# A graph network kernel: the in-degree product made inside the third tile period, a large accumulator for the last tile's gate product, and its gated rows converted at once

## The chip, the cores and the metric

The kernel runs on one core of a Trainium2 chip. The metric is the device time of one execution in microseconds (us); the time before is the median of three runs, 2218.25 us (2213.3 to 2223.8). The profile is of one further execution, of 2215.67 us; its span, from the first to the last recorded instruction, is 2213.9 us.

## The reference, cut to what matters

625 nodes have rows of 1024 numbers, and 10000 edges lead from `src` to `dst`. Two blocks follow each other, each a graph layer plus a linear attention, then a feed-forward part:

```
x = x + gat(ln(x)) + linear_attention_0(ln(x))
x = x + ternary_ffn(ln(x))                  # int8-like rows, three-valued weights
x = x + sage(ln(x)) + linear_attention_1(ln(x))
x = x + attention_and_experts(ln(x))
```

Two pieces matter here. The three-valued feed-forward part (`_L0_ffn_ref`) makes, for every row, a gate and an up product of 256 columns each from the rounded row, multiplies silu(gate) by up, rounds the result again, and multiplies it by `w_down`. The second graph layer (`_L1_gnn_ref`) takes a mean over incoming edges, so it needs `deg`, the count of edges into each node, and `1 / max(deg, 1)`.

## The kernel before, in words

All rows stay on the chip as five tiles (`NT = 5`) of 125 rows (`P`). The edges are turned once into a matrix of counts, `CT`, with sources on partitions and destinations along the free axis (626 columns, of which the last is padding). Right after it is made, one is added on its diagonal for the self-loops of the first graph layer.

The order of work is written out by hand: within the manual schedule each engine executes its instructions in the order in which the Python code emits them. The helper `do(prep, pe, after, after2)` (class `Stream`, line 189) emits first the waiting `after` steps of earlier calls, one step of each, and then the TensorE work `pe` of this call. So what evacuates a product is emitted one `do` later than the product, and a second step, `after2`, two later. Nearly all TensorE products are emitted by the helper `group`, so the profile gives them line 137 and they are told apart by the name of their accumulator.

PSUM is split into two kinds of accumulator: two small ones of one bank (`ps1`, line 63) and three large ones of two banks (`ps2`, line 67). A tile that is asked for waits on the chip until the earlier user of its buffer has been read.

The change lies in the loop over tile periods, `for p in range(NT + 2)` (line 1076), periods 0 to 6, called the first to the seventh here. It interleaves the first graph layer's softmax-weighted sums (`sums`, `turn_sums`, `up_again`) of tile p, the feed-forward part of tile p-1 (`ffn`, returning the steps p1, f1, f2, f3, f4, p5, f5) and the layer norm and transposition of tile p-2 (p5, f5, into `xnT1`). The steps of `ffn` are: p1 statistics and rounding; f1 eight transposes into `ptr`; f2 the gate and up product `pgu` and, one `do` later, tanh on ScalarE and the gated rows `sg` on VectorE; f3 two transposes into `phT` and, one `do` later, the conversion into `hT` (line 1017; the profile calls the shared tile that holds xq, qT, sg and hT `room`); f4 the product `pdn`, and one `do` later its addition into `x` (line 1033); p5 the next layer's norm (line 1040); f5 eight transposes (line 1048) and two ScalarE copies into `xnT1` (line 1049). `spacer` (line 1065) puts in between a key or value product of the second block's linear attention (`pk`, `pv`), which use large accumulators. A key product is followed by a VectorE addition `kb` (line 272), two ScalarE steps (`ke`, `kb`, lines 274 and 275), and as `after2` a VectorE step `kf` (line 280) that waits for them.

During the third period two large accumulators hold the unfinished output projections of tiles 2 and 4 (`px`), and the third one passes from `pdn` to the next user.

After the loop comes the second block's linear attention. Between two of its products `degrees()` (line 1143) takes the diagonal off `CT` again (five VectorE instructions), multiplies a matrix of ones by `CT` into `pdeg` (TensorE, 20 records in the profile), and one `do` later makes `dinv = max(degree, 1)` from `pdeg` and two checks: no count is over 4094, and the counts add up to the number of edges. If a check of this kind fails, the kernel runs its whole work once more in a slower form. `inverses()` then takes reciprocals.

Of the kernel before, what the change touches and what calls it, by code (L numbers as in the profile page):

```python
# [8 lines left out]
FP = mybir.dt.float32  # L9
# [4 lines left out]
AF = mybir.ActivationFunctionType  # L14
ALU = mybir.AluOpType
AX = mybir.AxisListType
# [3 lines left out]
N = 625  # L20
NT = 5
P = 125
NP = 626
HN = 313
E = 10000
# [13 lines left out]
MAGIC = 12582912.0  # L39
# [14 lines left out]
def attempt(ctx: ExitStack, tc: tile.TileContext, w: dict, out: bass.AP, shifted: bool):  # L54

    nc = tc.nc
# [6 lines left out]
    def ps1(name):  # L63
        pool, n = psums[-1]
        return pool.tile([128, 512], FP, tag="ps1", name=name, bufs=n)

    def ps2(name):
        return psums[-1][0].tile([128, 2, 512], FP, tag="ps2", name=name, bufs=3)


    ident = const.tile([128, 128], FP, name="ident")
# [5 lines left out]
    ones = const.tile([128, 128], FP, name="ones")  # L77
# [6 lines left out]
    inside = const.tile([128, 4], FP, name="inside")  # L84
# [49 lines left out]
    def group(dst, pairs):  # L134

        for i, (lhsT, rhs) in enumerate(pairs):
            made = nc.tensor.matmul(dst, lhsT=lhsT, rhs=rhs, start=(i == 0), stop=(i == len(pairs) - 1))  # L137
        latest["pe"] = made.ins.name
# [16 lines left out]
    def halves(ap):  # L155
        return ap.rearrange("p (h n) -> p h n", h=2)

    def nodes(t):
        return slice(t * P, (t + 1) * P)
# [26 lines left out]
    CT = CTr if shifted else CTr.bitcast(FP)  # L186
# [30 lines left out]
    mix = mixed_up.enter_context(tc.tile_pool(name="mix", bufs=1))  # L217
# [4 lines left out]
    do = Stream()  # L222
    hold = {}
# [139 lines left out]
    with ExitStack() as st0:  # L363
# [600 lines left out]
        def ffn(t):  # L964

            room = late.tile([128, 1536], FP, tag="room", name="room", bufs=1)
            xq = room[:P, 0:D]
            qT = room[:, D:D + KC * 64].bitcast(BF).rearrange("p (k n) -> p k n", k=KC)
            sg = room[:P, 0:256]
            hT = room[:, 256:384].bitcast(BF).rearrange("p (k n) -> p k n", k=2)  # L970
            xn1 = [mix.tile([128, NP], FP, tag="qf", name="xn1", bufs=2)[:P, 0:512] for h in range(2)]

            def p1():
                stats(t, mv0, rs0)
                nc.vector.tensor_scalar(xq, x[:, t, :], mv0[:, t, 0:1], rs0[:, t:t + 1],
                                        op0=ALU.subtract, op1=ALU.mult)
                quantise(xq, xq, rx[:, t:t + 1])

            def f1():
                def pe():  # L980
                    for h in range(2):
                        p = ps1("ptr").rearrange("p (c n) -> p c n", c=4)
                        for c in range(4):
                            k = 4 * h + c
                            nc.tensor.transpose(p[:, c, :P], xq[:, k * 128:(k + 1) * 128], ident[:P, :P])
                        nc.vector.tensor_scalar(qT[:, 4 * h:4 * h + 4, 0:P], p[:, :, :P], MAGIC, None,
                                                op0=ALU.subtract)

                do(None, pe)

            def f2():
                def pe():
                    hold["pgu"] = ps1("pgu")
                    group(hold["pgu"][:P], [(qT[:, k, 0:P], gu[:, k, :]) for k in range(KC)])

                def after():
                    pgu = hold["pgu"]
                    rgu = late.tile([P, 2], FP, tag="rgu", name="rgu", bufs=2)

                    nc.vector.tensor_scalar(rgu, wmean[:P, 0:2], rx[:, t:t + 1], None, op0=ALU.mult)  # L1000
                    nc.vector.tensor_scalar(rgu[:, 0:1], rgu[:, 0:1], 0.5, None, op0=ALU.mult)
                    nc.scalar.activation(sg, pgu[:P, 0:256], AF.Tanh, scale=rgu[:, 0:1])
                    nc.vector.scalar_tensor_tensor(sg, sg, 1.0, pgu[:P, 0:256], op0=ALU.add, op1=ALU.mult)
                    nc.vector.tensor_tensor(rgu[:, 1:2], rgu[:, 0:1], rgu[:, 1:2], op=ALU.mult)
                    nc.vector.scalar_tensor_tensor(sg, pgu[:P, 256:512], rgu[:, 1:2], sg, op0=ALU.mult, op1=ALU.mult)
                    quantise(sg, sg, rh[:, t:t + 1])

                do(None, pe, after)

            def f3():  # L1010
                def pe():
                    hold["ph"] = ps1("phT").rearrange("p (c n) -> p c n", c=4)
                    for c in range(2):
                        nc.tensor.transpose(hold["ph"][:, c, :P], sg[:, c * 128:(c + 1) * 128], ident[:P, :P])

                def after():
                    nc.vector.tensor_scalar(hT[:, :, 0:P], hold["ph"][:, 0:2, :P], MAGIC, None, op0=ALU.subtract)

                do(None, pe, after)

            def f4():
                def pe():
                    hold["pdn"] = ps2("pdn")
                    for c in range(2):
                        group(hold["pdn"][:P, c, :], [(hT[:, k, 0:P], dn[:, k, c * 512:(c + 1) * 512])
                                                   for k in range(2)])

                def after():
                    rd = late.tile([P, 1], FP, tag="rd", name="rd", bufs=2)
                    nc.vector.tensor_scalar(rd, wmean[:P, 2:3], rh[:, t:t + 1], None, op0=ALU.mult)  # L1030
                    for c in range(2):
                        xc = x[:, t, c * 512:(c + 1) * 512]
                        nc.vector.scalar_tensor_tensor(xc, hold["pdn"][:P, c, :], rd, xc, op0=ALU.mult, op1=ALU.add)

                do(None, pe, after)

            def p5():
                stats(t, mv1, rs1)
                for h in range(2):
                    nc.vector.tensor_scalar(xn1[h], x[:, t, h * 512:(h + 1) * 512], mv1[:, t, 0:1], rs1[:, t:t + 1],  # L1040
                                            op0=ALU.subtract, op1=ALU.mult)

            def f5():
                def pe():
                    for h in range(2):
                        p = ps1("ptr").rearrange("p (c n) -> p c n", c=4)
                        for c in range(4):
                            nc.tensor.transpose(p[:, c, :P], xn1[h][:, c * 128:(c + 1) * 128], ident[:P, :P])
                        nc.scalar.activation(xnT1[:, 4 * h:4 * h + 4, nodes(t)], p[:, :, :P], AF.Copy)

                do(None, pe)

            return p1, f1, f2, f3, f4, p5, f5


# [14 lines left out]
        def add_bias(*ts):  # L1070
            for t in ts:
                for c in range(2):
                    xc = x[:, t, c * 512:(c + 1) * 512]
                    nc.vector.tensor_tensor(xc, xc, kept[:, c, :] if t == 3 else bo[c][:P], op=ALU.add)

        for p in range(NT + 2):
            do()
            if p >= 2 and p != NT:
# [5 lines left out]
                mixed(4, cs=(0,))  # L1084
            if p == 2:
                add_bias(2, 4)
            if p >= 3:
                spacer()
            if p >= 2 and p != NT:
# [47 lines left out]
    sage = mixed_up.enter_context(tc.tile_pool(name="sage", bufs=1, reuse_waits="tile"))  # L1137
    dinv = sage.tile([128, NP], FP, name="dinv")
# [4 lines left out]
    def degrees():  # L1143
        for t in range(NT):
            nc.vector.tensor_tensor(CTr[:, t, nodes(t)], CT[:, t, nodes(t)], ident[:P, :P], op=ALU.subtract)

        def pe():
            pdeg = hold["pdeg"] = ps2("pdeg")
            for h in range(2):
                group(pdeg[:, h, :HN], [(ones[:P, :], CT[:, s, h * HN:(h + 1) * HN]) for s in range(NT)])  # L1150

        def after():
            nc.vector.tensor_scalar(halves(dinv), hold["pdeg"][:, :, :HN], 1.0, None, op0=ALU.max)
            if not shifted:
                most = sage.tile([128, 1], FP, name="most")
                nc.vector.tensor_reduce(most, dinv, AX.X, ALU.max)
                nc.vector.tensor_scalar(inside[:, 1:2], most, 4094.0, None, op0=ALU.is_le)

                nc.vector.tensor_reduce(most, hold["pdeg"][:, :, :HN], AX.XY, ALU.add)
                nc.vector.tensor_scalar(most, most, float(E), None, op0=ALU.is_equal)  # L1160
                nc.vector.tensor_tensor(inside[:, 1:2], inside[:, 1:2], most, op=ALU.mult)

        do(None, pe, after)

    def inverses():

# [73 lines left out]
    hT = []  # L1240
# [370 lines left out]
    hT = bigT("hT")  # L1611
# [384 lines left out]
```

## Time and profile before

| | |
|---|---|
| median of three runs | 2218.25 us |
| profiled execution, span | 2215.67 us, 2213.9 us |
| TensorE busy | 2113.7 us (95%) |
| VectorE, ScalarE, GpSimd busy | 713.6, 193.9, 340.0 us |
| mean granted TensorE clock | 0.979 |
| third period, first to first f5 transpose (489.65 to 525.20 us) | 35.55 us, granted clock 0.77 |
| fourth period (525.20 to 553.80 us) | 28.60 us, granted clock 1.00 |
| last tile to the seventh period's f5 (582.07 to 612.84 us) | 30.77 us, granted clock 0.83 |

PE is TensorE (its weight loads PEld), DVE is VectorE, ACT is ScalarE, POOL is GpSimd, SP the engine that issues most weight loads. In a timeline row the columns are start, length (or extent of merged neighbours), engine, line, operation, output and inputs, shapes, and in brackets the idle time of that engine before the row and who ended it. A float32 product is recorded as two matmuls for each one in the code. The granted clock is the share of full TensorE speed that the hardware allowed.

### The profile page before, as it was taken

How to read it: one execution, taken by the hardware profiler on the slowest of the kernel's cores; microseconds unless marked ns; L12 is line 12 of the kernel's file. 1: busy time of each engine (PE TensorE's matmuls, PEld its weight loads, DVE VectorE, ACT ScalarE, POOL GpSimd, SP SyncE). 2: the span in 40 equal slices, each digit the busy share in tenths (PEclk: the TensorE clock that was granted, in tenths of full speed). 3: DMA queues.
4: the chain of work that ended last, by engine and by line, in shares of the span. 5: the costliest groups of instructions: out<-in, count | busy, mean ns of one | idle time of the engine just before them, and what ended most of it. 6: DMA issues, size and time to landing. Idle time of an engine off the chain costs nothing. (4 is left out here: it accounts for less than half of the span.)

```text
span 2213.9 us, 17370 instructions
## 1 busy us (share of the span) xinstructions
PE 2113.7 (95%) x6934; PEld 1211.5 (55%) x6934; DVE 713.6 (32%) x1214; ACT 193.9 (9%) x354; POOL 340.0 (15%) x349
## 2 busy tenths in 40 slices
PE   8999899489899999999999999999999999999998
PEld 6565475255455777754446767457744444444443
DVE  5776378367532660000123133322011111111012
ACT  2000110012211100000000111100000000000000
POOL 1666656500000100210000000110000000000011
PEclk9999999789999999999999999999999999999999
DMA  7532263351122110240213111022099988997742
GB/s 221 201 101 82 79 199 104 74 155 33 39 86 76 48 38 1 86 149 32 76 38 105 38 38 38 28 96 89 8 362 344 330 309 294 330 330 285 277 141 91
DMA packets 145848, 301.62 MB, mean 136 GB/s; under 512 B 12370, under 2 KB 22436, under 8 KB 145754
## 3 DMA queue, kind: packets, MB, share of 16 engines
q1 hardware_dynamic: 123700, 244.23, 31.1%
q0 software_dynamic: 17376, 46.42, 7.0%
q10 hardware_dynamic: 4678, 9.72, 1.4%
q8 instruction: 58, 0.95, 0.2%
q14 instruction: 36, 0.29, 0.0%
HBM read 277.49 MB, written 22.84 MB: 136 GB/s over the span
## 5 line engine op out<-in xcount | busy, mean ns | idle before, releaser
L137 PE MATMUL pu<-w,xgT 128*128 128x512 f32 x768 | 333.9, 593 | 1.9 <-DVE xgT L1290 1.9
L137 PEld LDWEIGHTS pu<-w,xgT 128*128 128x128 f32 x768 | 144.0, 190 | 174.8 <-issue 172.0
L137 PE MATMUL pyb<-w,hb 128*128 128x512 f32 x384 | 174.3, 598 | 2.5 <-ACT yb L105 2.1
L137 PE MATMUL pq<-xnT,w 128*128 128x313 f32 x512 | 141.0, 435 | 7.0 <-DVE v L293 7.0
L137 PE MATMUL pv<-w,xnT 128*125 128x512 f32 x320 | 143.9, 600 | 3.7 <-issue 3.1
L137 PE MATMUL pk<-w,xnT 128*125 128x512 f32 x320 | 142.9, 598 | 1.8 <-issue 1.4
L137 PE MATMUL p<-tT,w 128*128 128x313 f32 x512 | 136.3, 428 | 0.4 <-DVE tT L1290 0.4
L137 PEld LDWEIGHTS pq<-xnT,w 128*128 128x128 f32 x512 | 98.9, 194 | 47.3 <-DVE v L293 7.8
L137 PEld LDWEIGHTS pyb<-w,hb 128*128 128x128 f32 x384 | 69.8, 189 | 90.9 <-issue 74.8
L1830 DVE TENSOR_TENSOR su<-pu,su 128x512 f32<-128x512 f32 x24 | 16.6, 691 | 314.6 <-ACT su L1829 314.6
L137 PEld LDWEIGHTS p<-tT,w 128*128 128x128 f32 x512 | 96.8, 190 | 37.9 <-issue 1.2
L137 PEld LDWEIGHTS pv<-w,xnT 128*125 128x125 f32 x320 | 60.2, 190 | 79.1 <-issue 77.4
L137 PEld LDWEIGHTS pk<-w,xnT 128*125 128x125 f32 x320 | 59.8, 189 | 73.9 <-issue 73.2
L641 POOL DMA_INDIRECT table<-es,at x79 | 84.6, 1071 | 61.2 <-issue 30.6
L1813 POOL DMA_INDIRECT xg<-rows_d,slots x12 | 11.3, 943 | 524.8 <-PE pxg L1820 449.0
L621 POOL DMA_INDIRECT ga<-xl_d,si x79 | 79.3, 1004 | 46.8 <-issue 21.6
L621 POOL DMA_INDIRECT gb<-xr_d,di x79 | 80.6, 1021 | 25.8 <-issue 25.8
L764 PE MATMUL px<-w,oT 128*125 128x512 f32 x160 | 69.8, 594 | 2.1 <-DVE x L933 1.4
L1179 DVE TENSOR_TENSOR z<-pz,z 125x512 fp32r<-125x512 f32 x10 | 6.9, 692 | 196.8 <-ACT z L1177 196.8
L137 PE MATMUL px<-w,hT 128*125 128x512 f32 x160 | 70.3, 592 | 0.0
L137 PE MATMUL px<-w,oT 128*125 128x512 f32 x160 | 70.3, 592 | 0.0
L137 PE MATMUL ph<-meanT,w 128*128 128x313 f32 x256 | 70.1, 426 | 0.0
(363 smaller groups left out, 2521.5 us busy)
## 6 DMA issues: line engine op xcount, KB each, us to landing
w<-in_eW_dram SPq DMA_DIRECT2D x144, 1024.0 KB
w<-in_L_Wk_dram SPq DMA_DIRECT2D x8, 1024.0 KB
w<-in_L_Wv_dram SPq DMA_DIRECT2D x8, 1024.0 KB
w<-in_L_Wq_dram SPq DMA_DIRECT2D x8, 1024.0 KB
w<-in_L_Wo_dram SPq DMA_DIRECT2D x8, 1024.0 KB
w<-in_W_self_dram SPq DMA_DIRECT2D x8, 1024.0 KB
w<-in_W_neigh_dram SPq DMA_DIRECT2D x8, 1024.0 KB
w<-in_sW_dram SPq DMA_DIRECT2D x8, 1024.0 KB
```

The source lines that it names most:

```text
L137: made = nc.tensor.matmul(dst, lhsT=lhsT, rhs=rhs, start=(i == 0), stop=(i == len(pairs) - 1))
L621: got = nc.gpsimd.indirect_dma_start(out=ab[g][side][0:p, j, :], out_offset=None, in_=src[:, :], in_offset=bass.IndirectOffsetOnAxis(ap=ix ...
L641: nc.gpsimd.indirect_dma_start(out=table[:, :], out_offset=bass.IndirectOffsetOnAxis(ap=at[0:p, lo + j:lo + j + 1], axis=0), in_=es[0:p, l ...
L764: made = nc.tensor.matmul(hold["px", t][:P, c, :], lhsT=oT[:, k, nodes(t)], rhs=wo[c](k), start=(k == 0), stop=(k == KC - 1 and keep is no ...
L1179: nc.vector.tensor_tensor(low, src, high.bitcast(FP), op=ALU.subtract)
L1813: nc.gpsimd.indirect_dma_start(out=xg, out_offset=None, in_=rows_d[:, :], in_offset=bass.IndirectOffsetOnAxis(ap=slots[:, b:b + 1], axis=0))
L1830: nc.vector.tensor_tensor(su, pu[:, 0, :], su, op=ALU.mult)
```

## The change

Three edits. First, the product of ones and `CT` leaves `degrees()`. It is made by a new function `in_degrees()` in the third period (p = 2), after `add_bias(2, 4)` and before the f5 step of tile 0, while the diagonal is still on `CT`. One `do` later, ScalarE copies it as 16-bit integers into a new SBUF tile `degree` of 128 x 626. `degrees()` now works from `degree`: it subtracts one for the diagonal, takes the maximum with one, and checks the sum against E + N. It no longer contains a `do` of its own. Second, for the last tile the gate product `pgu` takes half of a large accumulator in place of a small one. Third, f3 converts its two transposes into `hT` within its own `pe` step, ahead of what later `do` calls emit; this edit holds for all five tiles.

```diff
             def f2():
                 def pe():
-                    hold["pgu"] = ps1("pgu")
+                    hold["pgu"] = ps2("pgu")[:, 0, :] if t == NT - 1 else ps1("pgu")
...
             def f3():
                 def pe():
-                    hold["ph"] = ps1("phT").rearrange("p (c n) -> p c n", c=4)
+                    ph = ps1("phT").rearrange("p (c n) -> p c n", c=4)
                     for c in range(2):
-                        nc.tensor.transpose(hold["ph"][:, c, :P], sg[:, c * 128:(c + 1) * 128], ident[:P, :P])
-
-                def after():
-                    nc.vector.tensor_scalar(hT[:, :, 0:P], hold["ph"][:, 0:2, :P], MAGIC, None, op0=ALU.subtract)
-
-                do(None, pe, after)
+                        nc.tensor.transpose(ph[:, c, :P], sg[:, c * 128:(c + 1) * 128], ident[:P, :P])
+                    nc.vector.tensor_scalar(hT[:, :, 0:P], ph[:, 0:2, :P], MAGIC, None, op0=ALU.subtract)
+
+                do(None, pe)
...
+        degree = mix.tile([128, NP], mybir.dt.int16, tag="degree", name="degree", bufs=1)
+
+        def in_degrees():
+            def pe():
+                pdeg = hold["pdeg"] = ps2("pdeg")
+                for h in range(2):
+                    group(pdeg[:, h, :HN], [(ones[:P, :], CT[:, s, h * HN:(h + 1) * HN]) for s in range(NT)])
+
+            do(None, pe, lambda: nc.scalar.activation(halves(degree), hold["pdeg"][:, :, :HN], AF.Copy))
...
             if p == 2:
                 add_bias(2, 4)
+                in_degrees()
...
     def degrees():
         for t in range(NT):
             nc.vector.tensor_tensor(CTr[:, t, nodes(t)], CT[:, t, nodes(t)], ident[:P, :P], op=ALU.subtract)
-
-        def pe():
-            pdeg = hold["pdeg"] = ps2("pdeg")
-            for h in range(2):
-                group(pdeg[:, h, :HN], [(ones[:P, :], CT[:, s, h * HN:(h + 1) * HN]) for s in range(NT)])
-
-        def after():
-            nc.vector.tensor_scalar(halves(dinv), hold["pdeg"][:, :, :HN], 1.0, None, op0=ALU.max)
-            if not shifted:
-                most = sage.tile([128, 1], FP, name="most")
...
-                nc.vector.tensor_reduce(most, hold["pdeg"][:, :, :HN], AX.XY, ALU.add)
-                nc.vector.tensor_scalar(most, most, float(E), None, op0=ALU.is_equal)
...
-        do(None, pe, after)
+        nc.vector.tensor_scalar(dinv, degree, 1.0, 1.0, op0=ALU.subtract, op1=ALU.max)
+        if not shifted:
+            most = sage.tile([128, 1], FP, name="most")
...
+            nc.vector.tensor_reduce(most, degree, AX.X, ALU.add)
+            nc.vector.tensor_scalar(most, most, float(E + N), None, op0=ALU.is_equal)
```

More of the change, by code (lines that the diff above doesn't have):

```diff
@@ L1145, in degrees @@
             nc.vector.tensor_tensor(CTr[:, t, nodes(t)], CT[:, t, nodes(t)], ident[:P, :P], op=ALU.subtract)
-        def pe():
-            pdeg = hold["pdeg"] = ps2("pdeg")
-            for h in range(2):
-                group(pdeg[:, h, :HN], [(ones[:P, :], CT[:, s, h * HN:(h + 1) * HN]) for s in range(NT)])
-        def after():
-            nc.vector.tensor_scalar(halves(dinv), hold["pdeg"][:, :, :HN], 1.0, None, op0=ALU.max)
-            if not shifted:
-                most = sage.tile([128, 1], FP, name="most")
-                nc.vector.tensor_reduce(most, dinv, AX.X, ALU.max)
-                nc.vector.tensor_scalar(inside[:, 1:2], most, 4094.0, None, op0=ALU.is_le)
-                nc.vector.tensor_reduce(most, hold["pdeg"][:, :, :HN], AX.XY, ALU.add)
-                nc.vector.tensor_scalar(most, most, float(E), None, op0=ALU.is_equal)
-                nc.vector.tensor_tensor(inside[:, 1:2], inside[:, 1:2], most, op=ALU.mult)
-        do(None, pe, after)
+        nc.vector.tensor_scalar(dinv, degree, 1.0, 1.0, op0=ALU.subtract, op1=ALU.max)
+        if not shifted:
+            most = sage.tile([128, 1], FP, name="most")
+            nc.vector.tensor_reduce(most, dinv, AX.X, ALU.max)
+            nc.vector.tensor_scalar(inside[:, 1:2], most, 4094.0, None, op0=ALU.is_le)
+            nc.vector.tensor_reduce(most, degree, AX.X, ALU.add)
+            nc.vector.tensor_scalar(most, most, float(E + N), None, op0=ALU.is_equal)
+            nc.vector.tensor_tensor(inside[:, 1:2], inside[:, 1:2], most, op=ALU.mult)
     def inverses():
```

## The prediction

> **What bounds the kernel now.** I read the page first, then TensorE's waits and the busy time by stretch of the tile periods, then the timelines around each edit.
>
> ```profile
> span 2213.9 us, 17370 instructions
> PE 2113.7 (95%) x6934; PEld 1211.5 (55%) x6934; DVE 713.6 (32%) x1214; ACT 193.9 (9%) x354; POOL 340.0 (15%) x349
> ```
>
> TensorE is the bound: idle for only 100 us in all. The page's chain of waits reaches back over its last 3% only, so each stage has to be read by itself. From the tile periods on, an earlier TensorE is an earlier end: between 608 and 2000 us it is busy for 1382 of 1392 us, its few stalls come from VectorE (5.1 us for `oT`), none from a DMA, and SP's weight loads there wait for TensorE products (`pu` 319.5 us in total), so they move with it.
>
> Busy time by stretch (length; busy us of PE, PEld, DVE, ACT, POOL; granted clock; DMA share; GB/s), third period, fourth, last tile:
>
> ```profile
> 489.65:525.20 35.55, 34.25 (x113) 21.49 (x114) 25.68 (x51) 6.40 (x11) 3.27 (x6) 0.77 0.18 51
> 525.20:553.80 28.60, 27.27 (x114) 15.26 (x112) 21.33 (x43) 6.22 (x10) 0.00 (x0) 1.00 0.00 0
> 582.07:612.84 30.77, 23.80 (x63) 11.16 (x64) 12.54 (x30) 5.96 (x9) 0.00 (x0) 0.83 0.10 35
> ```
>
> The same work (113 and 114 matmuls) takes 35.55 us in the third period and 28.60 us in the fourth. The difference is the clock: 0.77 against 1.00. [...] The waits on TensorE between 436 and 652 us (total, times, longest):
>
> ```profile
> PE ptr L1048 <- DVE xn L1040: 5.3, 2, 4.0
> PE pdn L137 <- DVE room L1017: 3.4, 2, 2.9
> PE ptr L1048 <- ACT xnT L1049: 2.4, 1, 2.4
> ```
>
> Timeline of the third period:
>
> ```profile
> 484.58 1.02 PE L137 MATMUL pdn<-dn,room 128*125 128x512 bf16 x4 [1.32 <-DVE x L933]
> ...
> 485.64 1.41 DVE L1033 SCALAR_TENSOR_TENSOR x<-pdn,rd,x 125x512 f32<-125x512 f32 x2 [0.99 <-PE pdn L137]
> ...
> 489.65 1.93 PE L1048 MATMUL ptr<-ident,xn 125*128 125x125 f32 x8 [4.05 <-DVE xn L1040]
> ...
> 492.35 8.66 PE L137 MATMUL pg<-xl,pT 125*125 125x65 f32 x40 [0.77 <-ACT xnT L1049]
> ...
> 506.23 7.03 PE L137 MATMUL pk<-w,xnT 128*125 128x512 f32 x16
> ```
>
> A gap of 4.05 us, then `pg` at half speed (8.66 us; 4.58 in the fourth period). Full speed returns just before `pk`. The sixth period's tail:
>
> ```profile
> 589.72 0.65 PE L1048 MATMUL ptr<-ident,xn 125*128 125x125 f32 x4 [2.39 <-ACT xnT L1049]
> ...
> 598.97 0.69 DVE L272 TENSOR_TENSOR kb<-pk,bk_t 125x512 f32<-125x512 f32 x1 [7.51 <-PE pk L137]
> ...
> 601.02 0.69 DVE L280 SCALAR_TENSOR_TENSOR kf<-ke,kb 125x512 f32<-125x512 f32 x1 [1.36 <-ACT kb L275]
> 601.62 0.41 DVE L1017 TENSOR_SCALAR room<-phT 128x250 bf16<-128x250 f32 x1
> ...
> 602.09 1.97 PE L137 MATMUL pdn<-dn,room 128*125 128x512 bf16 x4 [2.95 <-DVE room L1017]
> 603.86 9.14 PE L137 MATMUL pv<-w,xnT 128*125 128x512 f32 x16
> 612.84 1.02 PE L1048 MATMUL ptr<-ident,xn 125*128 125x125 f32 x8
> ```
>
> `hT` (line 1017) stands behind `kf`, which waits for ScalarE; `pdn` waits for `hT`, and `pdn` and `pv` then run slow. The product to be moved:
>
> ```profile
> 646.46 5.43 PE L137 MATMUL pdeg<-CT,ones 125*128 125x313 f32 x20
> ...
> 651.73 7.03 PE L137 MATMUL pk<-w,xnT 128*125 128x512 f32 x16
> 651.93 0.81 DVE L1153 TENSOR_SCALAR dinv<-pdeg 128x626 f32<-128x626 f32 x1 [4.58 <-PE pdeg L137]
> ```
>
> It stands between products without a gap, so there it costs 651.73 - 646.46 = 5.27 us of the path.
>
> [...]
>
> **The change part by part**, against the profiled execution.
>
> *(a) `pdeg` leaves `degrees()`*: -5.27 us. VectorE's follow-up (0.81 + 0.81 + 0.15 + 0.81 + 0.15 + 0.16 = 2.9 us) moves to about 638.7 us, after the diagonal's removal, under `pv` (639.6 to 646.5 us). Behind it stand the two `kv` maskings, whose reader comes only at 728 us. `dinv` from 16-bit integers has no row; 0.3 to 0.81 us, taken as 0.81, hidden either way. Uncovered it would be 2.9 us.
>
> *(b) `pdeg` in the third period.* Two large accumulators are held for tiles 2 and 4, so it takes the one `pdn` leaves, free when line 1033 ends at 487.05 us. Start 487.1 us. The gap shrinks from 4.05 to 1.5 us; gaps of 1.43 and 1.32 us at 457.6 and 484.6 us slowed nothing, so I take full clock: 5.27 us, to 492.4 us. Queued behind it on TensorE: the `ptr` transposes, 2.7 us later than now (their input is ready at 490.05), then `pg` and all else. In the fourth period `ptr` to `pk` takes 534.48 - 525.19 = 9.29 us at full clock (now here 506.23 - 489.65 = 16.6). The new ScalarE copy (128 x 626; nearest row `hT` line 1257, 0.78 us; bounds 0.4 and 1.5) runs 492.6 to 493.4 us, ahead of the `xnT1` copies, the first of which could start at 493.0: +0.4 us (0 to 1.1). `pk` at 492.4 + 9.29 + 0.4 = 502.1 us: **-4.1 us**. The next user of that accumulator, this `pk`, finds it read long before. VectorE isn't the limit: its biases end at 497.7 us, `pg` at 498.6. If the clock drops under `pdeg` all the same, [...] at most 3.4 us lost, gain 0.7.
>
> *(c) `hT` before `kf`.* Fourth period: `pdn` begins at 545.70 after 0.44 us idle; `pv` behind it then waits for line 933, so -0.1. In the others `pdn` follows without waiting on it: 0. Sixth: `hT` right behind `kb`, 599.6 to 600.0, `pdn` at 600.05 in place of 602.09: -2.05 us. The gap behind `pk` falls from 2.95 to about 0.9 us, so I take the slow spell as gone: `pdn` and `pv` together 612.84 - 602.09 = 10.75 us now, 0.87 + 6.86 = 7.73 us at full clock (573.71 to 574.57 and 506.23 to 513.09 us): -3.0 (0 if a spell stays). The norm behind it would end at 606.3 us, before `ptr` at 607.8.
>
> *(d) `pgu` in a large accumulator*: the second four transposes need not wait 2.39 us, but `pk` still waits for the first ScalarE copy (589.09 to 589.67), which is behind tanh. `pk` at 589.75 in place of 590.20: -0.45 (0 to -2.4). The large accumulators of tile 4 and of `pdn` are free by then (575.1 and 576.8 us).
>
> None of the steps issues a DMA; SP's and POOL's queues are passed by none. Sum: -5.27 - 4.1 - 0.1 - 2.05 - 3.0 - 0.45 = **-15.0 us**. The profiled execution becomes 2200.7 us; the median, 2.6 us above it, 2203.2. I say **2203**.
>
> **The rivals.**
> 1. *The clock doesn't recover*: [...] For: after the sixth period's other gap the clock was at 0.5 from 592 to 594 us. [...] Gain 15.0 - 3.4 - 3.0 = 8.6: 2210 us.
> 2. *The product is only moved*: `ptr` waits 2.7 us and more behind `pdeg`, and the period is bound elsewhere (VectorE, 25.68 busy of 35.55 us), so (b) is 0: 2207 us.
> 3. *More warmth*: (d) also spares the slow spell at 591 us (1.7 us) and the ends of other spells fall well: 2198 us.
> 4. *Slower*: [...] `pdeg` waits for an accumulator that is freed late. Each us after 487.1 costs one; from 502 us on the whole gain is gone, and if it were freed only with tile 2's addition (518 us) it is 16 us slower: 2219 to 2234 us. Against: tile 2's sum is itself queued behind `pdeg`, so this would be a standstill, not a wait.
>
> **How the numbers follow.** About 0.5% (11.1 us, 2207.2) is what a measurement here can tell. Forecast 0.58 (own range 2197 to 2209, from the bounds above and the runs' spread of 10 us), rival 1 0.19, rival 2 0.11, rival 3 0.08, rival 4 0.04. Faster: 0.85 of the forecast, all of rival 3, a quarter of 1 and 2: 0.65. Slower 0.03; same 0.32. Range 2195 to 2212.
>
> **What would show it.** Right: `pdeg` begins 1.5 us after `pdn`, at full clock; the third period is about 29 us from `ptr` to `ptr`; `pdn` of the last tile starts about 1 us after `phT`; no `pdeg` after `kv`; mean clock about 0.984. Wrong: half clock under `pdeg`, `pg` at 8.7 us, or `pdn` still behind `kf`.

## The result, and the profile after

The changed kernel takes 2204.3 us (median of seven runs, 2200.8 to 2208.4). The kernel before, run beside it, takes 2217.45 us (seven runs, 2213.3 to 2223.8). The ratio is 0.9936, with a 95% interval of 0.9915 to 0.9956. The gain of 13.2 us is 0.6%, beyond the 0.5% named in the prediction; the forecast was 2203 us. The profiled execution is one of 2200.8 us, the fastest of the seven.

The first lines of its page are the span and the busy time of each engine:

```profile
span 2199.0 us, 17371 instructions
...
PE 2106.0 (96%) x6934; PEld 1205.2 (55%) x6934; DVE 713.1 (32%) x1214; ACT 194.7 (9%) x355; POOL 340.3 (15%) x349
```

TensorE executes as many matmuls as before. It is busy for 7.7 us less, because fewer of them run at half clock. The page's mean granted clock is 0.984 instead of 0.979.

The busy time by stretch has the columns of the prediction (length, busy time of five engines, granted clock, DMA share, GB/s). First the third period, from f5 transpose to f5 transpose, then the last tile from `pgu` to the next f5 transposes:

```profile
493.42:521.93 28.51, 27.06 (x113) 15.36 (x112) 23.17 (x46) 6.81 (x11) 3.28 (x6) 1.00 0.27 63
...
579.97:604.92 24.95, 20.84 (x55) 9.66 (x56) 11.26 (x28) 5.84 (x9) 0.00 (x0) 0.86 0.13 43
```

The third period takes 28.5 us at full clock, as the fourth did before; it was 35.55 us at 0.77. The last tile takes 24.95 us at a clock share of 0.86; before, from `pgu` at 583.49 us to the same transposes, it took 29.35 us at 0.83.

TensorE's waits between 430 and 652 us (total, times, longest) at the places that the change touches:

```profile
PE pdeg L137 <- DVE x L1031: 1.5, 1, 1.5
...
PE ptr L1046 <- DVE xn L1038: 1.3, 1, 1.3
...
PE pdn L137 <- DVE room L1015: 0.9, 1, 0.9
```

The 4.05 us gap ahead of the transposes is now 1.5 us ahead of `pdeg`, and the 2.95 us gap ahead of the last `pdn` is 0.9 us. The timeline of the third period shows how the product sits there:

```profile
485.52 1.02 PE L137 MATMUL pdn<-dn,room 128*125 128x512 bf16 x4 [1.32 <-DVE x L933]
...
488.05 5.54 PE L137 MATMUL pdeg<-CT,ones 125*128 125x313 f32 x20 [1.50 <-DVE x L1031]
...
493.42 1.02 PE L1046 MATMUL ptr<-ident,xn 125*128 125x125 f32 x8
493.62 0.69 ACT L1082 ACTIVATE degree<-pdeg 128x626 int16<-128x626 f32 x1 [0.86 <-PE pdeg L137]
...
494.85 4.58 PE L137 MATMUL pg<-xl,pT 125*125 125x65 f32 x40 [0.41 <-ACT xnT L1047]
...
502.96 7.03 PE L137 MATMUL pk<-w,xnT 128*125 128x512 f32 x16
```

`pdeg` runs at full speed (5.54 us, as in its old place within 0.11 us), the transposes follow it without a gap, and `pg` takes 4.58 us in place of 8.66. From `pdn` to `pk` it is 17.44 us now and was 21.65. The tail of the sixth period:

```profile
586.20 9.83 PE L137 MATMUL pk<-w,xnT 128*125 128x512 f32 x16 [1.94 <-ACT xnT L1047]
596.06 0.69 DVE L272 TENSOR_TENSOR kb<-pk,bk_t 125x512 f32<-125x512 f32 x1 [8.13 <-PE pk L137]
596.67 0.41 DVE L1015 TENSOR_SCALAR room<-phT 128x250 bf16<-128x250 f32 x1
...
597.14 1.08 PE L137 MATMUL pdn<-dn,room 128*125 128x512 bf16 x4 [0.90 <-DVE room L1015]
...
598.11 0.69 DVE L280 SCALAR_TENSOR_TENSOR kf<-ke,kb 125x512 f32<-125x512 f32 x1 [1.03 <-ACT kb L275]
```

The conversion of line 1015 now stands right behind `kb`, and `kf` comes 1.44 us after it. `pdn` starts 1.28 us after `phT` (595.86 us) instead of 3.32, and the stretch from `pdn` to the next transposes takes 7.78 us in place of 10.74. But `pk` takes 9.83 us, not 7.03: it starts at half clock, which the trace has from 584.83 to 591.66 us (granted clock 0.50). The old place of `pdeg`:

```profile
631.67 7.03 PE L137 MATMUL pv<-w,xnT 128*125 128x512 f32 x16
638.54 7.03 PE L137 MATMUL pk<-w,xnT 128*125 128x512 f32 x16
```

`pk` follows `pv` directly. Start to start it is 6.87 us; with `pdeg` between them it was 12.14.

Where the two profiled executions differ, summed from start to start along TensorE (the sum is the 14.9 us between the spans; starts are rounded, so a last digit can differ by one from the text):

| stretch | before | after | difference |
|---|---|---|---|
| start to the first `pg` | 437.57 | 438.51 | +0.94 |
| third period, `pdn` of the first tile to `pk` | 21.65 | 17.44 | -4.21 |
| that `pk` to the last tile's `pgu` | 77.26 | 77.00 | -0.26 |
| `pgu` to `pk` | 6.71 | 6.23 | -0.48 |
| `pk` to `phT` | 8.57 | 9.67 | +1.10 |
| `phT` to `pdn` | 3.33 | 1.27 | -2.06 |
| `pdn` to the seventh period's transposes | 10.74 | 7.78 | -2.96 |
| the `pv` and `pk` around the old place of `pdeg` | 12.14 | 6.87 | -5.27 |
| that `pk` to the second layer's `ph` | 175.88 | 174.45 | -1.43 |
| `ph` to the end | 1386.34 | 1386.06 | -0.28 |

The first `pdn` starts 47.01 us after the first `pg` in both, and `ptr` to `pv` is 26.75 us in both.

### The profile page after: what moved, and what is told of

Its sections match the earlier page's. It is cut to its first block, busy times and chain, and to the rows that moved or that the text cites. A ratio compares the mean times of both kernels' runs of the same rounds, so it can differ in the third digit from the quotient of the medians.

```text
span 2199.0 us, 17371 instructions
## 1 busy us (share of the span) xinstructions
PE 2106.0 (96%) x6934; PEld 1205.2 (55%) x6934; DVE 713.1 (32%) x1214; ACT 194.7 (9%) x355; POOL 340.3 (15%) x349
## 5 line engine op out<-in xcount | busy, mean ns | idle before, releaser
L137 PEld LDWEIGHTS pyb<-w,hb 128*128 128x128 f32 x384 | 69.8, 189 | 90.9 <-issue 74.8
L764 PE MATMUL px<-w,oT 128*125 128x512 f32 x160 | 69.8, 594 | 2.2 <-DVE x L933 1.6
```

The costliest lines, as they stand in the source:

```text
L764: made = nc.tensor.matmul(hold["px", t][:P, c, :], lhsT=oT[:, k, nodes(t)], rhs=wo[c](k), start=(k == 0), stop=(k == KC - 1 and keep is no ...
```

## Experiments

The theory is the prediction's sum: four separate gains. The rivals put to the test are that the clock falls again under the moved product; that the product is merely moved, so that any place in the third period would do; and that the gap's clock, not the product's old place, carries the gain. The kernels were run in three sets of four, each on its own chip: the three parts of the change alone and the filled gap on the first chip, the repeats of before and after, the copies first and the half-filled gap on the second, the others on the third. On the first chip, the stage ahead of the first `pg`, which the change doesn't touch, is at least 19 us shorter (`pg` at 416 to 419 us, and otherwise at 438 to 446 us). So a ratio is always taken to the kernel before on the same chip. The ratio comes from a comparison of all runs of a set, with a 95% interval; it isn't the quotient of the two medians, from which it differs by up to 0.13%. A gain in us is the difference of the medians.

In every trace I measured the same stretches, start to start, in us:

| kernel | `pdn` to `pk`, third period | last tile, `pgu` to `pk` | `pk` to `phT` | `phT` to `pdn` | `pdn` to `ptr` |
|---|---|---|---|---|---|
| before | 21.65 | 6.71 | 8.57 | 3.33 | 10.74 |
| after | 17.44 | 6.23 | 9.67 | 1.27 | 7.78 |
| product moved | 17.45 | 7.12 | 9.45 | 3.33 | 10.77 |
| rows converted at once | 21.85 | 7.12 | 9.00 | 1.28 | 7.78 |
| `pgu` in a large accumulator | 21.40 | 6.23 | 8.67 | 3.33 | 9.10 |
| gap filled, product kept | 17.44 | 7.12 | 9.24 | 3.33 | 7.78 |
| before, again | 21.50 | 6.71 | 8.56 | 3.33 | 7.78 |
| after, again | 20.48 | 6.23 | 8.66 | 1.27 | 7.78 |
| after, copies first | 17.45 | 4.52 | 6.97 | 1.27 | 7.78 |
| gap half filled | 22.13 | 7.12 | 8.94 | 3.33 | 7.78 |
| product moved behind `pk` | 21.88 | 7.12 | 8.97 | 3.33 | 7.78 |
| product moved, again | 19.14 | 7.12 | 9.40 | 3.32 | 10.74 |
| after, a third time | 20.47 | 6.23 | 8.67 | 1.27 | 7.78 |
| product in halves, copies first | 21.51 | 4.51 | 6.97 | 1.28 | 7.78 |

### The product moved, alone

`in_degrees()` and the new `degrees()` of the change, and nothing else.

```diff
                 add_bias(2, 4)
+                in_degrees()
```

> The move of the product alone: in-degree product in the third period, degrees() from the copied integers; gate product and hT as before. Theory (two gains, 5.27 us where the product stood and 4.2 us in the third period because the gap no longer halves the clock): 9.5 us faster than before, about 2208 us; from pdn of tile 0 to pk of the third period 17.4 us in place of 21.65. Rival (the product is only moved, the third period is bound elsewhere): 5.3 us faster, 21.6 us there. The last tile keeps its 2.95 us gap before pdn.

Measured on the first chip: 2187.48 us against 2192.79, ratio 0.9972 (0.996 to 0.9984), 5.3 us. The trace has both gains, 17.45 us in the third period and 6.87 us around the old place. The median gains only as much as the product's old place gives, the figure of the rival; the granted clock, compared under "The gap filled, the product kept", speaks against that rival all the same. The same kernel was run once more on the third chip.

> The move of the product alone once more, on the same chip as the whole change of this set. Theory: 9.5 us less in the two stretches when no slow spell falls on the product (pdn to pk 17.4 us), 6.5 us when one does (20.5 us): 6 to 10 us faster than before. Rival (the 5.3 us of the first set are all there is): 4 to 6 us.

There it is 2211.6 us against 2221.2, ratio 0.9955 (0.9939 to 0.997), 9.6 us, as the theory had it, although its third period in the trace is 19.14 us and so has gained less than in the first trace. The 5.27 us are in both traces; how much the gap adds to them isn't the same from execution to execution.

### The rows converted at once, alone

```diff
-                    hold["ph"] = ps1("phT").rearrange("p (c n) -> p c n", c=4)
+                    ph = ps1("phT").rearrange("p (c n) -> p c n", c=4)
...
+                    nc.vector.tensor_scalar(hT[:, :, 0:P], ph[:, 0:2, :P], MAGIC, None, op0=ALU.subtract)
...
-                do(None, pe, after)
+                do(None, pe)
```

> The early conversion into hT alone. Theory: 2.0 us of the gap before the last tile's pdn go, and 3.0 us more because pdn and pv run at full clock: 5 us faster, about 2212.5 us; phT to pdn of the last tile 1.3 us in place of 3.3, pdn to the next ptr 7.8 us in place of 10.75. Rival (the slow spell comes back with the gap before pk): phT to pdn 1.3 us, but pdn to ptr still over 10 us, 2 us faster. Third period and degrees as before.

Measured: 2189.78 us, ratio 0.998 (0.9972 to 0.9988), 3.0 us. `phT` to `pdn` is 1.28 us, the 2.05 us of the prediction to the digit, and no slow spell follows. The column `pdn` to `ptr` gives a reason why the time gains less than 5: of the eight traces that keep the old f3, only three have 10.7 us there and one has 9.10; the other four have the 7.78 us of full clock, with the 2.95 us gap just as it was. What isn't always there can't always be saved.

### The gate product in a large accumulator, alone

```diff
-                    hold["pgu"] = ps1("pgu")
+                    hold["pgu"] = ps2("pgu")[:, 0, :] if t == NT - 1 else ps1("pgu")
```

> The large accumulator for the last tile's gate product alone. Theory: the second four transposes run without a wait, but pk waits for the first copy on ScalarE behind tanh, so pgu to pk is 6.2 us in place of 6.7 and the time is 0.5 us less, not to be told from before (2217 us). Rival (the accumulator was the limit): pgu to pk 4.3 us, 2.4 us less and no slow spell under pk, 4 us in all.

Measured: 2191.29 us, ratio 0.9994 (0.9987 to 1.0), 1.5 us at the middle and none at the end of the interval. `pgu` to `pk` is 6.23 us: 0.48 less than in the two traces of the kernel before, and 0.89 less than in the six other traces without this edit. It never falls to 4.3. So the small accumulator isn't what holds `pk`; the queue on ScalarE is, which the next kernel tests.

### The copies ahead of tanh

This is the whole change, and in the last tile the f5 transposes and their two ScalarE copies are emitted at once, ahead of f2's tanh.

```diff
-            def f5():
-                def pe():
+            def f5_now():
...
                 if p == NT:
-                    made_of[p - 2][6]()
+                    made_of[p - 2][7]()
```

> The changed kernel, with the last period's four-and-four transposes and ScalarE copies of tile 3 put ahead of tanh of the last tile (one do earlier). Theory (pk there waits for ScalarE behind tanh and its table load, not for an accumulator): pgu to pk 4.1 us in place of 6.2, no slow spell under pk, so pk to phT 8.5 us in place of 9.7: 2 to 5 us faster than the whole change. Rival (tanh is now late and the gated rows with it): phT waits, 0 to 2 us slower than the whole change.

The timeline of the third period and of the last tile:

```profile
493.33 1.02 PE L137 MATMUL pdn<-dn,room 128*125 128x512 bf16 x4 [1.32 <-DVE x L933]
495.85 5.54 PE L137 MATMUL pdeg<-CT,ones 125*128 125x313 f32 x20 [1.50 <-DVE x L1031]
...
591.01 1.07 PE L1045 MATMUL ptr<-ident,xn 125*128 125x125 f32 x8 [1.28 <-DVE xn L1038]
591.66 1.07 ACT L1046 ACTIVATE xnT<-ptr 128x500 f32<-128x500 f32 x2 [1.58 <-PE ptr L1045]
592.31 7.13 PE L137 MATMUL pk<-w,xnT 128*125 128x512 f32 x16 [0.22 <-ACT xnT L1046]
592.75 1.28 ACT L1002 ACT_TABLE_LOAD   x1
```

In the changed kernel the copies began at 585.56 us, after the table load and tanh, and `pk` waited 1.94 us for them:

```profile
583.89 1.28 ACT L1002 ACT_TABLE_LOAD   x1 [1.64 <-DVE rgu L1001]
585.19 0.47 ACT L1002 ACTIVATE room<-pgu,rgu 125x256 f32<-125x256 f32 x1
585.56 1.06 ACT L1047 ACTIVATE xnT<-ptr 128x500 f32<-128x500 f32 x2
```

With the copies first they begin before the load, `pk` waits 0.22 us, and it runs without a slow spell (7.13 us). `pgu` to `pk` falls from 6.23 to 4.52 us and `pk` to `phT` from 8.66 to 6.97, 3.4 us together. The time is 2203.83 us against 2219.61, ratio 0.9916 (0.989 to 0.9941). The changed kernel in the same set has 2209.62, ratio 0.9944 (0.9923 to 0.9965). This is the fastest version by the medians of that set; the intervals overlap, so the times alone don't settle it.

### The gap filled, the product kept

The kernel before, with the new product written in the gap as well and left unused; `degrees()` is that of before. It does 5.27 us of extra TensorE work.

```diff
+                in_degrees()        # into pgap, copied to a tile that nothing reads
```

> The kernel before with the product added a second time, in the third period's gap, copied to SBUF and used by nobody; degrees() still makes its own. 20 records more work for TensorE. Theory (a filled gap keeps the clock): still 4.2 us faster than before, about 2213 us, with 17.4 us from pdn of tile 0 to pk. Rival (only the removal from degrees() pays): no gain, or up to 2.7 us slower, as ptr waits for the product.

Measured: 2192.48 us, ratio 0.9997 (0.9989 to 1.0005). The traced stretch is 4.2 us shorter with twenty more matmuls in it, as expected. The time shows no gain, only that the work costs nothing. The traced execution, 2189.11 us, is one of the two shortest of this kernel's thirteen, 3.4 us under their median. The mean granted clock, which is on record for every execution, tells more. On this chip it is on average 0.9815 in the kernel before (43 executions), 0.9842 with the product moved (six) and 0.9843 here. Taken as (1 - clock) x time, the slow spells cost about 41, 35 and 34 us; this is an estimate, since each clock is rounded to 0.001, which leaves about 1 us open. The rest of the time is 2152.6, 2152.9 and 2158.0 us. So the filled gap did spare some 6 us of slow clock, and the extra product, 5.3 us, used them up. And in the kernel with the product moved the gain is one of the clock, which a product that is merely moved would not show.

### Half of it

The same with the first ten of the twenty matmuls only (the edit is shown against the kernel with the filled gap).

```diff
-                for h in range(2):
-                    group(pdeg[:, h, :HN], [... for s in range(NT)])
+                group(pdeg[:, 0, :HN], [... for s in range(NT)])
```

> The kernel before with only half of the product (10 records, 2.64 us) added in the third period's gap, used by nobody; degrees() as before. It fits what is left of the gap behind the wait for the accumulator (487.1 to 489.75 us by the trace of before), so ptr starts no later. Theory (a filled gap keeps the clock): pdn to pk 14.8 us in place of 21.65, 6.8 us less there. Rival (half a fill is too little): the slow spell stays, 21.6 us there, no gain.

Measured: 2217.55 us, ratio 0.9988 (0.9972 to 1.0004); six of its 22 runs are at 2209.8 to 2211.7 us, the others from 2214 up. In the timeline:

```profile
493.84 2.90 PE L137 MATMUL pgap<-CT,ones 125*128 125x313 f32 x10 [1.50 <-DVE x L1033]
...
499.40 8.49 PE L137 MATMUL pg<-xl,pT 125*125 125x65 f32 x40 [1.81 <-ACT xnT L1049]
```

The fill is at full speed and covers its part of the gap, but a second gap of 1.81 us opens behind the transposes, and `pg` runs at half speed for all that. In this execution filling the gap wasn't enough: the granted clock is 1.00 until 499.62 us, behind the second gap, and 0.50 in the 3.41 us after it. The traced execution is one of 2220.19 us with a clock of 0.980. The six shortest have 0.981 to 0.983, so in them the spell may have stayed away; there is no trace of one.

### The product at another free place

The moved product, called after the third period's `pk` instead of in the gap.

```diff
             if 2 <= p <= NT:
                 spacer()
+            if p == 2:
+                in_degrees()
```

> The move alone, but to a busy place of the third period: behind the key product pk in place of the gap ahead of ptr. Theory (the gain in the third period is the filled gap, not the move): the gap and its slow spell stay (pdn of tile 0 to pk 21.5 us), the product costs its 5.3 us where it now stands (pk of the third period to pgu of the last tile 82.5 us in place of 77.2) and saves the same 5.3 us in degrees(): no difference to before, within 2 us. Rival (the third period has slack, any place in it is free): 5.3 us faster.

```profile
520.13 5.54 PE L137 MATMUL pdeg<-CT,ones 125*128 125x313 f32 x20 [1.17 <-DVE kb L272]
```

Measured: 2222.21 us against 2221.2, ratio 1.0003 (0.999 to 1.0016). The old place again gives 5.27 us. The new one costs more: it waits 1.17 us for the large accumulator that `kb` has to leave, and `pk` to `pgu` is 6.7 us longer (83.94 for 77.27). The gap ahead of the transposes keeps its slow spell (21.88 us from `pdn` to `pk`). So the rival of a free place anywhere falls: the place decides between the whole gain of the move and none.

### The kernel before and the changed one, again

> The kernel before, unchanged, as a control with its own trace on the chip of these runs. Theory: no difference; from pdn of tile 0 to pk of the third period 21.4 to 22 us[...]. Rival (on this chip the third period isn't slow, which would explain why the move alone gave 5.3 us and not 9.5): 17 to 19 us there.

Measured: the kernel before against itself has 2217.77 for 2219.61 us, ratio 0.9989 (0.9977 to 1.0001), so a per mille is no difference. In the trace `pdn` to `ptr` is 7.78 us where the first trace of the same kernel has 10.74; the gap of 2.95 us is there, and no slow spell follows:

```profile
604.98 1.08 PE L137 MATMUL pdn<-dn,room 128*125 128x512 bf16 x4 [2.95 <-DVE room L1017]
605.89 7.03 PE L137 MATMUL pv<-w,xnT 128*125 128x512 f32 x16
612.76 1.02 PE L1048 MATMUL ptr<-ident,xn 125*128 125x125 f32 x8
```

> The whole change on this chip. If the three parts add up as timed alone (5.3, 3.0 and 1.5 us): 9.8 us faster than before. If they add up as their own stretches in the traces say (9.5, 5.0 and 0.5 us): 15 us faster.

> The whole change once more, for a third trace and more times. Pooled over its sets it should stay 10 to 15 us faster than before. Theory: its times fall into those with 17.4 us from pdn to pk of the third period and those with 20.5 us[...].

The changed kernel has 0.9944 (0.9923 to 0.9965), 10.0 us, and then 0.9927 (0.9913 to 0.994), 17.4 us. Both traces have what the first one hadn't, a slow spell under `pdeg` (8.57 and 8.56 us in place of 5.54). The later one is of an execution of 2212.11 us with a clock of 0.979, the slowest of its six; the other five took 2203.1 to 2205.4 us at 0.982, so its spell isn't the rule there. In it:

```profile
493.35 1.02 PE L137 MATMUL pdn<-dn,room 128*125 128x512 bf16 x4 [1.31 <-DVE x L933]
495.88 8.56 PE L137 MATMUL pdeg<-CT,ones 125*128 125x313 f32 x20 [1.50 <-DVE x L1031]
```

These are the same instructions with the same gaps ahead, at nearly the same time from the start, as in the kernel with the copies first (493.33 and 495.85 us), where the product took 5.54 us. What differs between the two can't be the kernel's order here. The busy time by stretch in the second trace of the change, 3.41 us ahead of the fall of the clock and as much behind it:

```profile
489.82:493.23 3.41, 1.26 (x5) 0.54 (x4) 2.23 (x5) 0.00 (x0) 0.00 (x0) 1.00 0.32 121
493.23:496.65 3.42, 2.75 (x5) 1.85 (x6) 2.99 (x7) 0.29 (x1) 0.00 (x0) 0.50 0.00 0
```

The stretch of 3.41 us ahead of the drop holds `pdn`, the 1.3 us gap before it and a part of the 1.5 us gap behind it; TensorE is busy in it for 1.26 us. It runs at full clock, and the next 6.8 us, until 500.06 us, at half. In the traces of before and after, every half-clock spell is 3.41 us or a multiple of it long (3.41, 6.83, 17.07 and 44.37 us; but for a last one that runs on to the end of the span), and the three between 480 and 610 us in the kernel before begin at 488.63, 591.03 and 601.27 us, which is 30 and 3 times 3.413 us apart. So I cut a trace into stretches of 3.41 us, counted from its own spells. That is a way of reading the trace; what sets the clock was not shown. Cut so, the same instructions of the pair of timelines above fall into different stretches. In the third trace of the change, whose product ran slow, one stretch holds little but `pdn` (the columns are as before):

```profile
491.78:495.19 3.41, 1.28 (x5) 0.54 (x4) 2.21 (x5) 0.00 (x0) 0.00 (x0) 1.00 0.33 128
495.19:498.60 3.41, 2.72 (x5) 1.84 (x6) 2.98 (x7) 0.29 (x1) 0.00 (x0) 0.50 0.00 0
```

With the copies first the gaps are shared out over two stretches, and the clock stays at 1.00:

```profile
490.56:493.97 3.41, 2.09 (x7) 0.91 (x6) 2.62 (x5) 0.00 (x0) 0.00 (x0) 1.00 0.68 257
493.97:497.38 3.41, 1.91 (x8) 1.16 (x7) 2.81 (x5) 0.11 (x1) 0.00 (x0) 1.00 0.00 0
```

So the clock fell behind a stretch that was not idle: TensorE was busy for 37% of it (1.26 / 3.41) in the second trace and for 38% in the third.

### The product in halves on both sides of `pdn`

If the two gaps around `pdn` bring the spell together, filling both should keep the clock up: this was my estimate from the 1.26 and 1.28 us of work in the stretches above. Starting from the version with the copies first, the product is split over two small accumulators; the first half is made ahead of `pdn`, the second behind it.

```diff
             if p < NT:
                 up_again(p)
+            if p == 1:
+                in_degrees(0)
...
                 add_bias(2, 4)
-                in_degrees()
+                in_degrees(1)
```

> The changed kernel with the order of the last tile's copies ahead of tanh, and the in-degree product in two halves in the small accumulators: one half ahead of pdn of tile 0 (where TensorE waits 1.3 us for the accumulator), the other behind it, so that no wait of 1.5 us for a large accumulator is left. Theory: from pg of the first period to pk of the third 62.7 us in place of 64.5 (after) and 68.7 (before), no slow spell there in any execution; with the sixth period's gain about 20 us faster than before, 5 us or more faster than the whole change. Rival (pdn is 1.3 us later and with it the norm and ptr, which eats it): equal to the whole change in the third period.

```profile
487.27 2.80 PE L137 MATMUL pdeg<-CT,ones 125*128 125x313 f32 x10
491.57 0.62 PE L1045 MATMUL ptr<-ident,xn 125*128 125x125 f32 x4 [1.50 <-DVE xn L1038]
494.02 1.09 PE L1045 MATMUL ptr<-ident,xn 125*128 125x125 f32 x4 [1.83 <-ACT degree L1081]
```

Measured: 2206.38 us, ratio 0.9944 (0.9926 to 0.9962), no better than the changed kernel in the same set (0.9927). The gap ahead of `pdn` is filled, but behind the second half there is a gap of 1.50 us, and the second four transposes wait 1.83 us more, because the small accumulator that they need is free only after ScalarE has copied the half product. The slow spell moves to there (granted clock 0.50 from 493.02 to 496.43 us): the stretch is 21.51 us, as before the change, and from the first `pg` to the third period's `pk` it takes 69.8 us, not the expected 62.7. The large accumulator, which the change takes for the product, is what keeps the transposes free of this wait: in the trace of the change they follow `pdeg` (488.05 us, 5.54 us long) without a gap, at 493.42 us.

## Why the prediction came out right, and which of its terms were off

The forecast of 2203 us is 1.3 us from the median, and the profiled execution's 2200.8 us is what the sum gave. That agreement in the trace is in part luck, since it has three differences of chance that nearly cancel (+0.94, +1.10 and -1.43 us). Term by term:

- **(a) `pdeg` leaves its old place, -5.27 us.** Right: the step from `pv` to `pk` is 6.87 us in all eight traces with the new `degrees()`, wherever they make the product, and 12.14 us in the six others. VectorE's follow-up is hidden; `dinv` from 16-bit integers, the row that was missing, takes 0.48 us (taken as 0.81).
- **(b) `pdeg` in the gap, -4.1 us.** The place, the start 1.5 us after `pdn` and the wait of the transposes are right. ScalarE's copy takes 0.69 us (taken as 0.78), and `pg` waits 0.41 us for what stands behind it. The step that failed is "gaps of 1.43 and 1.32 us ... slowed nothing, so I take full clock". It held in four of the seven traces with the whole product in the gap (17.44 or 17.45 us); the other three have 19.14, 20.48 and 20.47. Their mean is 18.55, and the mean of the five traces with nothing in that gap is 21.66 (21.65, 21.50, 21.85, 21.40, 21.88). So the term is -3.1 us on average of these traces. I had looked at each gap by itself; in the second trace of the change 3.41 us take in most of two. In stretches of that length, the emptiest one at the two gaps holds 1.91 us of TensorE's work in the first trace of the change and in the kernel with the copies first, which stay fast, and 1.26, 1.28 and 1.55 us in the three traces that don't.
- **(c) `hT` before `kf`, -2.05, -3.0 and -0.1 us.** The first is right in all six traces with the edit. The second was mis-sized: I read the slow spell from one execution and took it as always there. Without the edit, eight traces have 10.74, 10.77, 10.74, 9.10 and four times 7.78 us, on average 9.06; with it, all six have 7.78. The term is -1.3 us. The stretch of 3.41 us with the 2.95 us gap holds 1.30 us of TensorE's work in the kernel before, where the clock falls to 0.50 behind it, and 1.45 us in the same kernel run again, where it stays at 1.00. The third is -0.26 us: `pk` to `pgu` is 77.01 us with this edit alone and 77.27 with that of `pgu` alone.
- **(d) `pgu` in a large accumulator, -0.45 us.** The reason, that `pk` still waits for the copies behind tanh, is right, and the kernel with the copies first shows it. The size is 0.48 to 0.89 us, on average 0.8 (7.02 in the eight traces without the edit, 6.23 in the four with it alone or with the whole change).

With the measured averages the sum is 5.27 + 3.1 + 2.05 + 1.3 + 0.26 + 0.8 = 12.8 us. The whole change was timed three times, with 13.2, 10.0 and 17.4 us. They scatter by more than the 1.3 us between the forecast and the median, so that this nearness is luck as well.

The trace of before shows two more things of the spell in the third period. It begins at 488.63 us, in the gap itself and 1.02 us ahead of the transposes, behind a stretch with 0.38 us of work. And it goes on under a busy TensorE: three stretches of 3.41 us that are nearly full (3.11, 3.41 and 3.23 us), mostly of `pg` with its 65 columns, have the clock at 0.50:

```profile
485.22:488.63 3.41, 0.38 (x2) 0.00 (x0) 2.81 (x5) 0.11 (x1) 0.00 (x0) 1.00 0.00 0
...
492.04:495.46 3.42, 3.11 (x15) 3.12 (x16) 3.27 (x6) 0.73 (x2) 0.00 (x0) 0.50 0.00 0
495.46:498.87 3.41, 3.41 (x18) 3.41 (x18) 2.24 (x4) 0.00 (x0) 1.27 (x3) 0.50 0.00 0
498.87:502.28 3.41, 3.23 (x17) 2.86 (x17) 1.16 (x4) 0.00 (x0) 0.97 (x2) 0.50 0.44 154
```

That spell lasts 17.07 us, to 505.70 us. Under `pdeg`, with 313 columns, it lasted 6.83 us in the second trace of the change (493.23 to 500.06 us). The product took 7.22, 8.56 and 8.57 us in the three traces with a spell there, 1.7 to 3.0 us more than the 5.54 us of full clock; the 3.4 us that the prediction allowed for that case were an estimate. So with the product in the gap less was lost even where the clock fell: `pdn` to `pk` took 19.14, 20.47 and 20.48 us there, and 21.66 us on average with nothing in the gap.

Of the rivals, the first (the clock falls again) isn't an alternative to the forecast: it is what some executions do. Two of the three traces of the changed kernel have the spell under `pdeg`. The second (merely moved) falls with the third period's 28.5 us; it is true of another place, after `pk`, where the move gains nothing. The third (more warmth under the last `pk`) didn't come: `pk` to `phT` stayed at 8.7 to 9.7 us in the traces of the change. The fourth falls as well: the accumulator is free when `pdeg` needs it, while after `pk` it is not (1.17 us).

Open is the following. On the first chip the three parts gained 5.3 + 3.0 + 1.5 = 9.8 us, as much as the smallest gain of the whole change in its three sets (13.2, 10.0 and 17.4 us); the whole change was not run there. Also open is why the slow spells cost only some 6 us less there with the gap filled or the product moved, when a spell of 17.07 us, which at its clock of 0.50 I estimate to be worth up to half its length (8.5 us), is gone from both traces. Slow spells at other places, which differ from execution to execution, would explain both, but with one trace for each kernel and set that is an argument and not shown.

## What to carry to other kernels

A slow clock spell behind a short gap was paid in a share of the executions here (three of the seven traces with the whole product in the gap, four of the eight with the old f3 in the last tile): weigh it by that share from several traces, and add up the busy time of TensorE around a gap, over the length of the shortest slow spell of the traces (3.41 us here), in place of judging the gap alone. That sum gave no threshold: around one gap it ordered the traces that were cut so (1.26 to 1.55 us with a spell, 1.91 us without), from one gap to the other it did not (1.45 us without). Work moved into such a gap is worth what it cost in its old place, in every trace here (5.27 us), and what the gap's slow spell cost, sometimes; at another place that looks as free it cost all that it saved (ratio 1.0003). When a matmul waits for ScalarE, look at what stands ahead of the copy in ScalarE's order (here a table load of 1.28 us and tanh of 0.47 us) before giving it another accumulator.

## What the runs showed of the hardware that I had not expected

- The clock fell behind a stretch in which TensorE was busy for more than a third of the time: 1.26 of 3.41 us in the second trace of the change. In the first trace of the change, two such stretches with 2.10 and 1.91 us (482.43 to 485.85 and 485.85 to 489.26 us, around the same gaps) were followed by a clock of 1.00. Busy time alone doesn't order the traces: the clock stayed at 1.00 behind 1.45 us in the sixth period of the kernel before, run again (600.58 to 604.00 us), and fell to 0.50 behind 1.55 us (product moved, again, 489.64 to 493.05 us) and 1.60 us (gap half filled, 496.21 to 499.62 us) in the third period.
- A clock that had fallen stayed down for different lengths of TensorE work: in the third period of before, `pg`, 40 records of 65 columns, ran 8.66 us at half clock inside a spell of 17.07 us; under `pk` in the sixth period, records of 512 columns, the spell was over after 3.41 us (591.03 to 594.44 us).
- Two executions with the same instructions at times that agree within 0.03 us ran the same product in 5.54 and in 8.56 us.
- The same program took about 27 us less in the set on the first chip than on the other two (2192.8 against 2219.6 and 2221.2 us at the median), at least 19 us of it ahead of the first `pg` (416.4 to 418.6 us there, 438.2 to 446.3 on the other two).
